# A graph layer on one core: gathered columns tied to TensorE's progress

## The chip, the cores and the metric

The kernel runs on one core of one Trainium2 chip. The metric is device time in microseconds of one execution, as the median of repeated runs. The page and the trace describe one profiled execution of the same program.

## The reference

One layer of a graph network with 6,250 nodes of 64 features and 206,250 edges, whose end nodes `dst` are sorted. For each edge the normalised row of its source node is added to the edge's attributes, the sum goes through a relu, and the results are summed by end node; then come two small matrix products.

```python
h = jnp.maximum(_layernorm(x, axis=-1), 0.0)
msg = jax.nn.relu(h[src] + edge_attr)
agg = jax.ops.segment_sum(msg, dst, num_segments=x.shape[0])
g = h + agg
g = jax.nn.relu(g @ W1 + b1)
return x + (g @ W2 + b2)
```

## The kernel before

The edges are cut into 269 groups (`NG` = 268 full ones and a tail) of 128 partitions by 6 columns (`G`), so a group holds 768 edges. Each edge needs the row of its source node, and the kernel gets these rows in two ways. Three of a group's six columns (`G - H`) are fetched by GpSimd: `gather` issues one indirect DMA for each column, which takes 128 rows of `h_rows` (the normalised nodes, in DRAM) by the indices in `src_sb`, into a tile `xg`. The other three columns (`H`) are worked out by TensorE from a copy of all nodes that stays on the chip (`hp`): `find` and `back` (VectorE, with a part on ScalarE) build 0/1 tables, `slots_of` (L487) multiplies them with `hp` into a half bank, `slots_out` (L495, ScalarE) copies the result to `picked`, and `pick` (L502) sorts the rows to the edges in a PSUM bank, on top of the attributes that `room` (L510) has copied there. Twelve groups (`WHOLE`) have all six columns done by TensorE; they are two units each and nothing is gathered for them. All other groups from the sixth on (`F0` = 5) are one unit. The first five groups are gathered in full.

`half(u)` issues one unit: it enters the group `AHEAD` = 9 groups later (`enter`, `load`: the attributes by SP's DMA queue, the gathered columns by GpSimd's), then `window_sum(u - 1)` (L600, the sums by node of the unit before), `room`, three calls of `slots_of` for the next set (20, 16 and 16 matmuls of L487) with two `slots_out`, `pick(u + 1)` (18 matmuls of L502), `sum_into_z` (L563), `messages` (L585 adds the gathered columns to the attributes, L588 adds up the picked ones, L590 is the relu), the third `slots_out`, and the one-hot of L569 by which `window_sum` sums. A set is two units, so which `slots_of` comes in which unit is written out by hand. Preparations for later sets (`rank_at`, `rank_count`, `rank_of`, `rank_turn`, `source`) are spread over the units by `chunk`.

The schedule is manual: each engine executes its instructions in the order in which they are issued in the code, and an instruction waits by semaphores only for what it reads and overwrites. GpSimd's queue holds nearly nothing but gathers, so before the change a gather waits only for its turn, for its indices and rows, and for its `xg` tile (twelve of them), whose last reader is L585. GpSimd thus works ahead of the other engines as far as there are free tiles.

Before the units comes a stage that normalises the nodes (`ln_head`, `ln_rows`, `ln_turn`, `ln_parts`) and a loop over the first five groups, which are entered, added, summed by node, and mixed with the first preparations: `rank_count` (L279 and L281, counts, copied by L283), `source` (L331, copied by L334) and `window_sum`.

Of the kernel before, what the change touches and what calls it, by code (L numbers as in the profile page):

```python
# [19 lines left out]
N, E, D = 6250, 206250, 64  # L20
P = 128
G = 6
# [17 lines left out]
AHEAD = 9  # L40
# [4 lines left out]
H = 3  # L45
PP, RR = 128, 49
# [4 lines left out]
S = 32  # L51
J = P // S
assert PARTS * BB == RR - 1 and PP == P and PARTS % J == 0
Q = PARTS * S // P
# [3 lines left out]
RAW = 3  # L58
F0 = 5
# [22 lines left out]
def kernel(  # L82
# [14 lines left out]
    nc = tc.nc  # L97
# [9 lines left out]
    src_sb = const.tile([P, CP], I32, name="src_sb")  # L107
# [56 lines left out]
    ones_b = const.tile([P, P], F16, name="ones_b")  # L164
# [13 lines left out]
    hp = const.tile([PP, RR, 3, D], BF16, name="hp")  # L178

    h_rows = dram.tile([NP, D], F32, name="h_rows")  # L180
# [14 lines left out]
                              in_=edge_attr[C * P:(C + TJ) * P, :].rearrange("(p j) d -> p (j d)", j=TJ))  # L195
            nc.sync.dma_start(out=ea[:, G - 1, :], in_=edge_attr[E - P:, :])

    def gather(xg, idx, n, rows):
        for j in range(n):
            nc.gpsimd.indirect_dma_start(  # L200
                out=xg[:, j, :], out_offset=None, in_=rows[:, :],
                in_offset=bass.IndirectOffsetOnAxis(ap=idx[:, j:j + 1], axis=0))

    def first_col(g):
        return 0 if g < NG else G - CT
# [4 lines left out]
    def pool_cols(g):  # L210
        return G if g < F0 else 0 if is_whole(g) else G - H

    def load(g):
        ea = eas[g % LOOK]
        attr_load(ea[:, :G], g)
        lo, hi = first_col(g), pool_cols(g)
        if is_whole(g):
            return ea, None
        if g < F0:
            xg = lnp.tile([P, G, D], F32, name="xr", bufs=F0)  # L220
        else:
            xg = edge.tile([P, G - H, D], F32, name="xg")
        gather(xg[:, lo:], src_sb[:, g * G + lo:g * G + hi], hi - lo, x if g < RAW else h_rows)
        return ea, xg

    loaded = [load(g) for g in range(RAW)]
# [49 lines left out]
    def rank_count(c):  # L276
        ps = psum.tile([P, RG, PARTS, H], F32, name="rows", bufs=1)
        at = ats[c]
        nc.tensor.matmul(ps, upper, at, start=True, stop=False)  # L279
        for d in range(1, H):  # L280
            nc.tensor.matmul(ps[:, :, :, d:], ones_b, at[:, :, :, :H - d], start=False, stop=(d == H - 1))  # L281
        counts[c] = rank.tile([P, RG, PARTS, H], F16, name="before", bufs=1)
        nc.scalar.copy(counts[c], ps)  # L283

# [39 lines left out]
    def source(c):  # L324
        n = RG // 2
        ps = psum.tile([n * S, 2, n * S], F32, name="rows", bufs=1)
        mk, oh = marks.pop(c), holds.pop(c)
        for u in range(2):
            for t in range(H):
                row = lambda a: a[:, u * n:(u + 1) * n, :, t].rearrange("p g s -> p (g s)")  # L330
                nc.tensor.matmul(ps[:, u], row(mk), row(oh), start=(t == 0), stop=(t == H - 1))  # L331
        col = rank.tile([PARTS, RG * S], I16, name="source")
        for i in range(n):
            nc.scalar.copy(col.rearrange("m (u i s) -> m u i s", u=2, s=S)[:, :, i],  # L334
                           ps[i * S:i * S + PARTS, :, i * S:(i + 1) * S])
        lines[c] = dram.tile([SETS, PARTS, 2 * S], I16, name="source_row", bufs=3)
        nc.sync.dma_start(out=lines[c].rearrange("k m s -> m k s"), in_=col.rearrange("m (k s) -> m k s", k=SETS))
# [101 lines left out]
    backs, sources, spots, found, picked, halves, picks = {}, {}, {}, {}, {}, {}, {}  # L439

    def source_load(k):
        sources[k] = rank.tile([P, PARTS * 2 * S], I16, name="sources")
        nc.sync.dma_start(out=sources[k][:PP], in_=lines[k // SETS][k % SETS].rearrange("(o m) s -> o (m s)", o=1)
                          .to_broadcast([PP, PARTS * 2 * S]))
# [34 lines left out]
    def slots_of(k, n0):  # L479
        ps = next_half()[:, :2 * 3 * D].rearrange("p (u d) -> p u d", u=2)  # L480
        for u in range(2):
            i, q = divmod(n0 + u, Q)
            sets = BB + 1 if q == 0 else BB
            for b in range(sets):
                for j in range(J):
                    m = (b * PARTS + q * J) + j if b < BB else BB * PARTS + j
                    nc.tensor.matmul(ps[j * S:(j + 1) * S, u], found[k][:, m, i, :],  # L487
                                     hp[:, min(m, RR - 1)].rearrange("p t d -> p (t d)"),
                                     start=(b == 0), stop=(b == sets - 1))
        if n0 == 0:  # L490
            picked[k] = hot.tile([P, 2 * Q, 3 * D], BF16, name="picked")
        halves[k, n0] = ps

    def slots_out(k, n0):
        nc.scalar.copy(picked[k][:, n0:n0 + 2], halves.pop((k, n0)))  # L495

    def pick(u0, cols):
        k, i = divmod(u0, 2)
        ps = picks[u0]
        for u in cols:  # L500
            for q in range(Q):
                nc.tensor.matmul(ps[:, u, :3].rearrange("p t d -> p (t d)"), backs[k][:, q, i * H + u, :],  # L502
                                 picked[k][:, i * Q + q], start=False, stop=(q == Q - 1), skip_group_check=True)

    def room(u):
        g, c0 = UNITS[u]
# [54 lines left out]
    def sum_into_z(u):  # L561
        at = window_start(group_of(u))
        nc.vector.tensor_tensor(z[:, ds(at, W)], z[:, ds(at, W)], aggs.pop(u), ALU.add)  # L563
# [7 lines left out]
            slots.unsqueeze(1).to_broadcast([P, n, W]), ALU.is_equal)  # L571
        hots[u] = oh

    def enter(g):
        if g <= NG and g not in taken:
            taken[g] = loaded[g] if g < RAW else load(g)

    def messages(u):
        g, (lo, hi) = group_of(u), span(u)
# [15 lines left out]
    def window_sum(u):  # L595
        (lo, hi), oh, msg = span(u), hots.pop(u), msgs.pop(u)
        pa = half_banks[u % 3][:, 2 * 3 * D + u // 3 % AB * W:][:, :W]
        for j in range(lo, hi):
            i = (j - lo) % 2
            nc.tensor.matmul(pa[i * D:(i + 1) * D], msg[:, j, :], oh[:, j, :], start=(j < lo + 2), stop=(j >= hi - 2))  # L600
        aggs[u] = pa

    xbs = {}
# [57 lines left out]
    def half(u):  # L661
        g = group_of(u)
        k, i = divmod(u, 2)
        first = ((0, 2), (6, 8))[i]
        later = ((4,), (10,))[i]
        now = is_set(k + 1)
        if is_first(u):
            enter(g + AHEAD)
        if i == 0:
            if is_set(k + 3):  # L670
                source_load(k + 3)
        elif is_set(k + 3):
            spot_load(k + 3)
        window_sum(u - 1)
        if u + 1 < U:
            room(u + 1)
        if now:
            for n0 in first:
                slots_of(k + 1, n0)
                slots_out(k + 1, n0)  # L680
            for n0 in later:
                slots_of(k + 1, n0)
        if u + 1 < U:
            pick(u + 1, range(H))
        sum_into_z(u - LAG)
        blocks_behind(u - LAG)
        messages(u)
        if now:
            for n0 in later:
                slots_out(k + 1, n0)  # L690
        one_hot(u)
        if i == 0:
            if is_set(k + 1):
                back_near(k + 1)
                back(k + 1, 3, Q)
            if is_set(k + 2):
                find(k + 2, 0)
                find(k + 2, BB)
        else:
            if is_set(k + 2):  # L700
                back_far(k + 2)
                back(k + 2, 0, 3)
                find(k + 2, 1)
        chunk(u + 14, rank_at)
        chunk(u + 13, rank_count)
        chunk(u + 12, rank_of)
        chunk(u + 11, rank_marks)
        chunk(u + 11, rank_turn)
        chunk(u + 10, rank_holds)
        chunk(u + 10, rank_fits)  # L710
        chunk(u + 9, source)
        if g in CHECKS and is_first(u):
            find_left(CHECKS.index(g))
# [50 lines left out]
    slots_of_edges()  # L764
    ln_turn(*rows[-1])
    rank_fits(0)
    for g in range(AHEAD):
        enter(g)
    places(2, NCH)
    for k in (0, 1):  # L770
# [3 lines left out]
    for g in range(F0):  # L774
        for i in range(g * LOOK // F0, (g + 1) * LOOK // F0):
            tails_begin(i)
        enter(g + AHEAD)
        messages(g - F0)
        one_hot(g - F0)
        if g == 0:  # L780
            rank_at(1)
            rank_count(1)
        if g == 1:
            rank_of(1)
            rank_marks(1)
            rank_turn(1)
        if g == 2:
            rank_holds(1)
            rank_fits(1)
            source(1)  # L790
        if g == 3:
            rank_at(2)
            rank_count(2)
        if g >= 1:
            window_sum(g - 1 - F0)
        if g > LAG:
            sum_into_z(g - LAG - 1 - F0)
    sum_into_z(-LAG - 1)
    while split:
        fill()  # L800
# [6 lines left out]
    back(0, 0, Q)  # L807
    back_near(0)
    for n0 in range(0, 2 * Q, 2):
        slots_of(0, n0)  # L810
        slots_out(0, n0)
    source_load(2)
    spot_load(2)
    room(0)
    pick(0, range(H))
    for b in range(BB + 1):
        find(1, b)
    back_far(1)
# [87 lines left out]
```

## Time and profile before

| | us |
|---|---|
| median of 3 runs | 1706.47 |
| lowest, highest run | 1706.32, 1710.89 |
| profiled execution | 1700.59 |
| its span, from the first to the last instruction | 1698.9 |
| TensorE matmuls busy | 1226.6 (72%) |
| TensorE weight loads busy | 957.5 (56%) |
| VectorE busy | 995.5 (59%) |
| ScalarE busy | 954.9 (56%) |
| GpSimd busy | 785.4 (46%) |
| mean granted TensorE clock | 0.914 |

The busy times come from the first part of the page. PE is TensorE's matmuls, PEld its weight loads, DVE VectorE, ACT ScalarE, POOL GpSimd and SP SyncE. In the rows, a line such as L585 is the line of the kernel that issued the instruction. "<-" behind the idle time of an instruction names what ended the wait before it; "issue" is time in which nothing that the profile shows was waited for, and "remote" a signal that the profile cannot put down to an instruction. In a timeline row, neighbouring instructions of one kind are merged and counted with x.

### The profile page before, as it was taken

What the parts mean: (1) busy time and instruction counts of PE and PEld (TensorE: products, weight loads), DVE (VectorE), ACT (ScalarE), POOL (GpSimd) and SP (SyncE); (2) the same over time, 40 slices, a digit from 0 to 9 for tenths busy, and PEclk for the clock granted to TensorE, in tenths of its full rate; (3) what the DMA queues carried; (4) which work ended last, traced back from release to release, by engine and by line L of the source; (5) the groups of instructions that cost most, each with busy time, mean ns of one, the idle gap of its engine ahead of it and who ended that gap; (6) DMA issues with size and microseconds to landing.
All of it is one profiled execution on the core that took longest, in us unless ns stands there. A gap on an engine that the chain in (4) does not pass through costs nothing. (4 is left out here: it accounts for less than half of the span.)

```text
span 1698.9 us, 54613 instructions
## 1 busy us (share of the span) xinstructions
PE 1226.6 (72%) x23185; PEld 957.5 (56%) x23185; DVE 995.5 (59%) x2686; ACT 954.9 (56%) x1979; POOL 785.4 (46%) x798
## 2 busy tenths in 40 slices
PE   3047777777777777877777777777777777777786
PEld 2036565655556566656556555655655565565665
DVE  7446556656566555655656555655556555565565
ACT  4335555556556555555655655655555555565664
POOL 6734544553453543554455454444444544545510
PEclk8569999899999998899999999988999999999998
DMA  5213433334333433334333433433334333434330
GB/s 182 70 51 104 110 96 105 108 96 111 102 97 107 112 104 93 107 94 118 105 104 102 109 103 98 105 106 103 96 102 106 98 106 106 109 98 109 106 95 25
DMA packets 115095, 172.34 MB, mean 101 GB/s; under 512 B 28444, under 2 KB 83613, under 8 KB 114845
## 3 DMA queue, kind: packets, MB, share of 16 engines
q1 hardware_dynamic: 89752, 143.03, 28.2%
q0 software_dynamic: 25088, 25.74, 8.5%
q8 instruction: 184, 3.01, 0.7%
q14 instruction: 67, 0.54, 0.1%
q10 hardware_dynamic: 4, 0.01, 0.0%
HBM read 164.85 MB, written 3.84 MB: 99 GB/s over the span
## 5 line engine op out<-in xcount | busy, mean ns | idle before, releaser
L200 POOL DMA_INDIRECT xg<-h_rows,src_sb x754 | 749.9, 995 | 827.6 <-DVE ea L585 662.4
L487 PE MATMUL half<-hp,found 128*32 128x192 bf16 x14352 | 509.6, 256 | 267.3 <-issue 243.3
L495 ACT CAST picked<-half 128x384 bf16<-128x384 f32 x828 | 365.2, 475 | 344.3 <-PE half L487 300.2
L487 PEld LDWEIGHTS <-found 128*32 128x32 bf16 x14352 | 325.2, 98 | 393.6 <-issue 357.1
L502 PE MATMUL pick<-picked,backs 128*128 128x192 bf16 x4968 | 519.1, 266 | 3.5 <-ACT pick L510 2.1
L502 PEld LDWEIGHTS <-backs 128*128 128x128 bf16 x4968 | 449.3, 106 | 60.5 <-issue 50.7
L563 DVE TENSOR_TENSOR z<-z,half 128x32 f32 x281 | 53.0, 189 | 638.4 <-ACT picked L495 511.1
L590 ACT ACTIVATE msg<-ea 128x384 f32<-128x384 f32 (+2 forms) x281 | 142.9, 509 | 259.2 <-DVE ea L588 199.1
L474 DVE TENSOR_SCALAR backs<-spots,ids 128x768 bf16<-128x768 int16 x690 | 279.9, 453 | 0.0
L600 PE MATMUL half<-oh,msg 128*64 128x32 f32 x3224 | 152.7, 229 | 109.5 <-ACT picked L495 57.5
L600 PEld LDWEIGHTS half<-oh,msg 128*64 128x64 f32 x3224 | 121.3, 140 | 171.8 <-ACT picked L495 75.1
L455 DVE TENSOR_SCALAR found<-sources,nodes_of 128x1536 bf16<-128x1536 int16 (+1 forms) x414 | 211.4, 537 | 0.1
L588 DVE TENSOR_REDUCE ea<-pick 128x192 f32<-128x576 f32 x276 | 207.1, 750 | 0.1
L510 ACT COPY pick<-ea 128x576 f32<-128x576 f32 x264 | 168.4, 638 | 0.0
L467 ACT ACTIVATE backs<-dist,ones 128x768 bf16<-128x768 bf16 x138 | 129.3, 937 | 0.3 <-ACT dist L464 0.3
L464 ACT ACTIVATE dist<-spots,far 128x768 bf16<-128x768 int16 x138 | 129.2, 936 | 0.0
L569 DVE TENSOR_TENSOR oh<-slot,slots 128x192 f32<-128x192 int16 (+2 forms) x281 | 95.4, 340 | 36.9 <-remote 36.9
L585 DVE TENSOR_TENSOR ea<-ea,xg 128x192 f32<-128x192 f32 x252 | 90.0, 357 | 1.8 <-issue 1.3
L279 PE MATMUL rows<-at,upper 128*128 128x432 f16 x46 | 16.5, 358 | 49.1 <-remote 28.4
L283 ACT CAST before<-rows 128x432 f16<-128x432 f32 x46 | 23.4, 510 | 35.7 <-remote 31.8
L331 PE MATMUL rows<-holds,marks 128*96 128x96 f16 x276 | 25.9, 232 | 11.4 <-DVE oh L569 5.0
L334 ACT CAST source<-rows 24x64 int16<-24x64 f32 x138 | 27.5, 199 | 8.5 <-remote 5.3
(107 smaller groups left out, 439.7 us busy)
## 6 DMA issues: line engine op xcount, KB each, us to landing
sources<-source_row SPq DMA_DIRECT2D x138, 384.0 KB
ea<-in_edge_attr_dram SPq DMA_DIRECT2D x268, 192.0 KB
spots<-spot_rows SPq DMA_DIRECT2D x138, 192.0 KB
xg<-h_rows,src_sb POOLq DMA_INDIRECT x754
xb<-in_x_dram SPq DMA_DIRECT2D x12, 128.0 KB
out_dram<-o SPq DMA_DIRECT2D x12, 128.0 KB
h_rows<-x SPq DMA_DIRECT2D x3, 384.0 KB
dst_sb<-in_dst_main_dram SPq DMA_DIRECT2D x1, 804.0 KB
```

Of the source, the lines that this page charges most:

```text
L200: nc.gpsimd.indirect_dma_start(out=xg[:, j, :], out_offset=None, in_=rows[:, :], in_offset=bass.IndirectOffsetOnAxis(ap=idx[:, j:j + 1], a ...
L455: nc.vector.tensor_scalar(found[k][:, b * PARTS:b * PARTS + n].rearrange("p m i s -> p (m i s)"), sources[k][:, :n * 2 * S], nodes_of[:, b ...
L464: nc.scalar.activation(dists[k], spots[k].bitcast(I16), AF.Abs, bias=far)
L467: nc.scalar.activation(backs[k][:, Q - 1].rearrange("p t s -> p (t s)"), dists.pop(k), AF.Relu, bias=ones[:, 0:1], scale=-1.0)
L474: nc.vector.tensor_scalar(backs[k][:, q].rearrange("p t s -> p (t s)"), spots[k].bitcast(I16), ids[:, q:q + 1], None, op0=ALU.is_equal)
L487: nc.tensor.matmul(ps[j * S:(j + 1) * S, u], found[k][:, m, i, :], hp[:, min(m, RR - 1)].rearrange("p t d -> p (t d)"), start=(b == 0), st ...
L495: nc.scalar.copy(picked[k][:, n0:n0 + 2], halves.pop((k, n0)))
L502: nc.tensor.matmul(ps[:, u, :3].rearrange("p t d -> p (t d)"), backs[k][:, q, i * H + u, :], picked[k][:, i * Q + q], start=False, stop=(q ...
L510: nc.scalar.copy(picks[u][:, :H, :3], parts)
L588: nc.vector.tensor_reduce(ea[:, c0:c0 + H], picks.pop(u)[:, :H, :3].rearrange("p j t d -> p j d t"), AX.X, ALU.add)
L590: nc.scalar.activation(msg[:, lo:hi], ea[:, lo:hi], AF.Relu)
L600: nc.tensor.matmul(pa[i * D:(i + 1) * D], msg[:, j, :], oh[:, j, :], start=(j < lo + 2), stop=(j >= hi - 2))
```

## The change

The list `beats` collects matmul instructions of TensorE as they are issued. `gather` takes a tuple `behind` of such instructions, and ties its last `len(behind)` columns to them, one each: the indirect DMA of a column waits for its matmul's completion. In the units, `half(u)` enters group `g + 9` with the last three marks: the end of the first `slots_of`, the end of the third, and the end of the `pick` of the unit before. Before the units, groups 0 to 6 are entered at once without waits (before: 0 to 8), and groups 7 to 13 one or two at the end of each pass of the loop over the first five groups, with their last two columns behind the last two marks of that time: counts, sources and sums by node. Groups 14 and later are entered by the units as before, now with marks.

```diff
+    beats = []
+    beat = mybir.DependencyInfo(mybir.DependencyClass.Sync, mybir.DependencyReason.ANTI)
+
+    def gather(xg, idx, n, rows, behind=()):
         for j in range(n):
-            nc.gpsimd.indirect_dma_start(
+            it = nc.gpsimd.indirect_dma_start(
...
+            if j >= n - len(behind):
+                tc.add_manual_dep(it.ins, behind[j - n + len(behind)].ins.name, beat, reason="pace")
...
 (rank_count) if c < 3: beats.append(last)
 (source)     if c < 2: beats.append(last)
 (window_sum) if u < -1: beats.append(last)
...
-    def enter(g):
+    def enter(g, behind=()):
         if g <= NG and g not in taken:
-            taken[g] = loaded[g] if g < RAW else load(g)
+            taken[g] = loaded[g] if g < RAW else load(g, behind[first_col(g):])
...
         if is_first(u):
-            enter(g + AHEAD)
+            enter(g + AHEAD, beats[-G + H:])
...
             for n0 in first:
-                slots_of(k + 1, n0)
+                begun = slots_of(k + 1, n0)
                 slots_out(k + 1, n0)
+                if n0 == first[0]:
+                    beats.append(begun)
             for n0 in later:
-                slots_of(k + 1, n0)
+                beats.append(slots_of(k + 1, n0))
         if u + 1 < U:
-            pick(u + 1, range(H))
+            beats.append(pick(u + 1, range(H)))
...
-    for g in range(AHEAD):
+    for g in range(F0 + 2):
         enter(g)
...
-        enter(g + AHEAD)
         messages(g - F0)
...
         if g > LAG:
             sum_into_z(g - LAG - 1 - F0)
+        for e in ((7,), (8,), (9,), (10, 11), (12, 13))[g]:
+            enter(e, beats[-2:])
...
     for n0 in range(0, 2 * Q, 2):
-        slots_of(0, n0)
+        begun = slots_of(0, n0)
         slots_out(0, n0)
+        if n0 % 4 == 0 and n0:
+            beats.append(begun)
...
-    pick(0, range(H))
+    beats.append(pick(0, range(H)))
```

The three lines in brackets stand for the same step in three functions, which also keep their last matmul in `last`; `slots_of` and `pick` return theirs.

## The prediction

> **What bounds the kernel now.** The page comes first: no engine is full (TensorE is busy 72% of the span), so the time is in the waits. The row that stands out is GpSimd's:
>
> ```profile
> span 1698.9 us, 54613 instructions
> L200 POOL DMA_INDIRECT xg<-h_rows,src_sb x754 | 749.9, 995 | 827.6 <-DVE ea L585 662.4
> ```
>
> 754 gathers of about 1 us, which start when VectorE's addition of L585 has freed a tile. I then took one unit from the timeline. Columns: start, length, engine, line, operation, and in brackets the idle time before it and what ended it.
>
> ```profile
> 601.20 1.66 PE L502 MATMUL pick<-picked,backs 128*128 128x192 bf16 x18
> 602.13 0.94 POOL L200 DMA_INDIRECT xg<-h_rows,src_sb  x1 [1.86 <-DVE ea L585]
> 603.14 0.54 PE L600 MATMUL half<-oh,msg 128*64 128x32 f32 x12 [0.27 <-issue]
> 603.37 1.02 POOL L200 DMA_INDIRECT xg<-h_rows,src_sb  x1 [0.30 <-issue]
> 603.61 0.90 PE L487 MATMUL half<-hp,found 128*32 128x192 bf16 x32
> 604.70 0.95 POOL L200 DMA_INDIRECT xg<-h_rows,src_sb  x1 [0.30 <-issue]
> 604.98 0.29 PE L487 MATMUL half<-hp,found 128*32 128x192 bf16 x3 [0.47 <-issue]
> 605.72 0.24 PE L487 MATMUL half<-hp,found 128*32 128x192 bf16 x1 [0.45 <-issue]
> 606.44 0.85 PE L487 MATMUL half<-hp,found 128*32 128x192 bf16 x16 [0.48 <-issue]
> 606.58 0.86 ACT L495 CAST picked<-half 128x384 bf16<-128x384 f32 x2 [1.76 <-PE half L487]
> 607.09 0.19 DVE L563 TENSOR_TENSOR z<-z,half 128x32 f32 x1 [1.65 <-ACT picked L495]
> 607.22 2.71 PE L502 MATMUL pick<-picked,backs 128*128 128x192 bf16 x18
> 607.27 0.36 DVE L585 TENSOR_TENSOR ea<-ea,xg 128x192 f32<-128x192 f32 x1
> 607.90 0.94 POOL L200 DMA_INDIRECT xg<-h_rows,src_sb  x1 [2.25 <-DVE ea L585]
> ...
> 610.63 0.95 POOL L200 DMA_INDIRECT xg<-h_rows,src_sb  x1 [0.31 <-issue]
> ...
> 612.45 0.86 ACT L495 CAST picked<-half 128x384 bf16<-128x384 f32 x2 [1.54 <-PE half L487]
> ```
>
> Three gathers run back to back (602.13, 603.37, 604.70). TensorE starts the 52 matmuls of L487 at 603.61, breaks off after 32, and does the last 16 only at 606.44. The first copy of L495 needs the first 20 of the 52, which are over by 604.51, yet it begins at 606.58, 1.88 us after the third gather began. In the next unit it begins at 612.45, 1.82 us after that unit's third (610.63). VectorE (L563, L585) and the next gathers follow from that copy, so it closes the loop. The counter-example is a whole group, for which nothing is gathered:
>
> ```profile
> 151.92 0.75 DVE L588 TENSOR_REDUCE ea<-pick 128x192 f32<-128x576 f32 x1
> 153.57 1.26 PE L487 MATMUL half<-hp,found 128*32 128x192 bf16 x52
> 154.74 0.85 ACT L495 CAST picked<-half 128x384 bf16<-128x384 f32 x2
> 155.79 0.75 DVE L588 TENSOR_REDUCE ea<-pick 128x192 f32<-128x576 f32 x1
> ...
> 148.04:155.79 7.75, 7.25 (x161) 6.17 (x160) 6.33 (x19) 6.19 (x13) 0.00 (x0) 1.00 0.34 97
> ...
> L588 DVE TENSOR_REDUCE ea<-pick x262: 748/750/759, 118.8 to 1628.5; 128x192 f32<-128x576 f32 x131
> L200 POOL DMA_INDIRECT xg<-h_rows,src_sb x718: 939/946/1286, 119.1 to 1628.9; - x180
> ```
>
> Here the 52 matmuls are one run and the two units without gathers take 7.75 us together, 3.88 each (window row: start:end, length, busy times by engine). The last two rows (one line's instructions from 118 us on) give the mean: 261 units between 118.8 and 1628.5, of which 718/3 = 239 with three gathers and 22 without; (1509.7 - 22 x 3.88)/239 = 5.96 us. So three gathers go with 2.08 us more per unit, 497 us in all. That is the bound I go by: a series of gathers keeps back TensorE's signals, and some of its instructions, until about 1.85 us after its last one began.
>
> The same stands in the stage before the units, where 36 gathers ran one after the other:
>
> ```profile
> 52.64 0.95 POOL L200 DMA_INDIRECT xg<-h_rows,src_sb  x1 [0.30 <-issue]
> 62.20 0.86 PE L600 MATMUL half<-oh,msg 128*64 128x32 f32 x12
> 69.48 0.94 POOL L200 DMA_INDIRECT xg<-h_rows,src_sb  x1 [0.30 <-issue]
> 90.54 0.36 DVE L569 TENSOR_TENSOR oh<-slot,slots 128x192 f32<-128x192 int16 x1 [28.43 <-remote]
> 91.72 0.80 PE L281 MATMUL rows<-at,ones_b 128*128 128x288 f16 x2
> 97.00 0.95 POOL L200 DMA_INDIRECT xg<-h_rows,src_sb  x1 [0.30 <-issue]
> 100.34 0.52 ACT L283 CAST before<-rows 128x432 f16<-128x432 f32 x1 [31.83 <-remote]
> 109.03 3.27 PE L487 MATMUL half<-hp,found 128*32 128x192 bf16 x68 [13.25 <-DVE found L455]
> ```
>
> The sums by node of L600 are through at 63.06, but the one-hot that needs their buffer starts at 90.54, 27.5 us later; the counts of L281 are through at 92.52, their copy starts at 100.34.
>
> But not every signal is late:
>
> ```profile
> 609.14 1.18 POOL L200 DMA_INDIRECT xg<-h_rows,src_sb  x1 [0.30 <-issue]
> 609.86 0.23 PE L317 MATMUL rows<-ident_b,spot_i 128*18 128x128 bf16 x1
> 610.12 0.26 ACT L319 COPY sp<-rows 18x128 bf16<-18x128 bf16 x1
> ...
> 1628.87 0.95 POOL L200 DMA_INDIRECT xg<-h_rows,src_sb  x1 [2.33 <-DVE ea L585]
> ...
> 1631.39 1.26 PE L487 MATMUL half<-hp,found 128*32 128x192 bf16 x52
> ```
>
> Between a unit's second and third gather, 0.98 us after the second began, a signal arrives at once (609.86 + 0.23, used at 610.12). Behind the only gather that stands alone (1628.87), the 52 run unbroken. So the hold comes late in a series: after about two gathers, until 1.85 us past the last.
>
> **The change part by part.** *In the units.* Nothing is computed more or less; three matmuls a unit gain a signal and each gather waits for one. Column 0 waits for the first 20 matmuls of L487, column 1 for the last 16, column 2 for the pick of L502, all of the unit before. These gathers get into tiles freed two groups earlier (12 tiles, now fetched ten groups ahead), so L585 no longer releases them. Call the moment of the first L495 copy T (606.58). Today the first gather starts at 607.90, T + 1.32. From the end of L585 (607.63) to that start it takes 0.27 us; the same after a TensorE signal, and 0.03 for a second wait instruction, makes T + 0.30. The signals of columns 1 and 2 do not delay their gathers: the last 16 end at 607.29, T + 0.7, the pick (0.64 after T, 1.66 long) at T + 2.3, while GpSimd, at the spacing of 602.13 to 604.70, comes to the third only at T + 0.30 + 2.57 = T + 2.87. So the series stays back to back but begins 1.02 us earlier in the unit. The hold then ends at T + 2.87 + 1.85 = T + 4.72, later than the 3.88 a unit needs by itself, so it still sets the unit. Today the same sum is 1.32 + 2.57 + 1.85 = 5.74 against 5.78 measured (606.58 to the next T would be 5.87). Gain: 1.02 x 239 = 244 us.
>
> Bounds of this term: if the hold disappears, a unit is 3.88 plus the addition of L585, 0.36, that whole groups lack: 4.24, a gain of 1.72 x 239 = 411. If picks stay as slow as at 607.22 (2.71 instead of 1.66), the pick ends at T + 3.35, the third gather starts at T + 3.65, and the unit is 5.50: a gain of 0.46 x 239 = 110. I take the middle value since 1.66 is the pick behind an unheld stretch. The granted clock was 1.00 in the stretch without gathers. The Trainium skill (TensorE: Matmul & The Clock Gate, "What's actually happening") halves the clock after an idle window of about 3.4 us; by that rule no unit, before or after, would have the slow pick and the sum is 244; the row of 2.71 behind gaps far shorter than that speaks against relying on it.
>
> *What waits behind it.* On GpSimd only gathers are queued, so a waiting gather delays gathers alone; their reader, L585, comes ten groups later, 47 us at 4.7 us. SP's queue keeps its order in the units; before them the loads of groups 7 to 13 come after those of sources and spots, free, since they are needed from the third unit on.
>
> *Before the units.* Groups 7 to 13 (10 is whole) are entered one by one with columns 1 and 2 behind TensorE's last two marks; groups 14 to 17 move into the units. GpSimd would run as now up to column 1 of group 9 (69.48), then wait for the very sums of L600 started at 62.20. The series stops, the hold ends at 69.48 + 1.85 = 71.3, and the one-hot of 90.54 starts 19.2 us earlier. The counts end 2.0 us later (73.3); two gathers (71.6, 72.85) hold them to 74.7, 1.4 us instead of 7.8: 6.4 more. From the copy (100.34) to the first unit work (109.03) lies real work, unchanged. Sum 25 us, between 0 and 26. The 12 gathers moved into the units make four more units of the gathered kind: 4 x (4.94 - 3.88) = 4 us back, 4.94 being 5.96 - 1.02.
>
> Sum: the profiled execution took 1700.6 us (span 1698.9 + 1.7); 1700.6 - 244 - 25 + 4 = 1436. The median of the runs, 1706.5, lies 0.35% above it. I say 1430.
>
> **The rivals.** *Spread, they hold nothing* (0.16): waits put enough room between gathers that each behaves like that of 1628.87. For: that row. Against: by the sum above GpSimd is the late one and the series stays closed. 1700.6 - 411 - 21 = 1268.
>
> *The hold moves along* (0.13): it is paid per gather wherever it begins, the units stay at 5.96, only the stage before them gains: 1680. For: 2.08/3 = 0.69 us per gather, near the gaps of 0.7 us between the starts at 604.98, 605.72 and 606.44. Against: the unheld 52 at 1631.39.
>
> *Gathers wait for their own hold* (0.15), slower: if a single gather keeps back TensorE's signal for the full 1.85 us, each next column can start only 1.85 + 0.30 after the one before. A unit becomes 0.30 + 2 x 2.15 + 1.85 = 6.45, 0.49 more in 243 units: +119 - 25 = 1795. It decides once the hold begins less than 0.4 us after a gather starts (the last 16 signal at T + 0.7). Against: the signal at 610.09 came through 0.95 us into one.
>
> *The order of gathers is nothing to TensorE* (0.04): its gaps come from its own issue, as their label says, and both stages stay: 1700. The Trainium skill (SBUF — State Buffer, "SBUF: two separate sides") has TensorE on ports of its own, waiting on nobody, which speaks for this. The units of 3.88 us speak against it.
>
> **How the numbers follow.** The forecast has 0.52, its own range 1330 (units of 4.5) to 1570 (slow picks). The rivals have 0.16, 0.13, 0.15, 0.04. From 1255 to 1685 the range holds the forecast and the first two rivals, 0.81. Faster by over 0.3% (about what a measurement of this kernel can tell): 0.52 + 0.16 + 0.13 = 0.81; within 0.3%: 0.04; slower: 0.15.
>
> **What would show it.** Right: gathers released by PE L487 and L502 rather than L585; the first of a unit about 0.3 us after the L495 copy begins; units near 4.7 us; L487 still broken, but shorter; L495 still some 1.85 us behind the third gather; first L487 near 84 us instead of 109; picks mostly 1.66. Wrong: units at 3.9 to 4.3 with unbroken runs of 52 (first rival), at 5.8 (second), or above 6 with GpSimd idle between columns for 2 us (third).

## The result and the profile after

| | before | after |
|---|---|---|
| median of 4 runs, us | 1706.39 | 1530.7 |
| lowest to highest, us | 1702.1 to 1710.89 | 1529.74 to 1531.52 |
| span of the profiled execution, us | 1698.9 | 1528.6 |
| mean granted TensorE clock | 0.914 | 0.945 |

The ratio after to before is 0.897, 95% interval 0.8946 to 0.8994. The change gains 176 us where 276 were forecast: the time lies inside the range, 101 us above the number. The direction held; one step of the mechanism behind the number, as the experiments will show, did not.

The lines of the code have moved: the gather is now L204, `slots_of` L497, `slots_out` L506, `pick` L513, the addition into `z` L575, the addition of the gathered columns L597, the reduction L600, the sums by node L612. From the page after (busy time, mean ns of one, idle time before it and what ended most of it):

```profile
span 1528.6 us, 55110 instructions
L204 POOL DMA_INDIRECT xg<-h_rows,src_sb x754 | 746.1, 990 | 678.6 <-PE half L497 552.5
L497 PE MATMUL half<-hp,found 128*32 128x192 bf16 x14352 | 442.1, 256 | 112.6 <-issue 57.9
L513 PE MATMUL pick<-picked,backs 128*128 128x192 bf16 x4968 | 486.4, 255 | 3.5 <-ACT pick L522 2.1
```

Gathers are now released by `slots_of` on TensorE instead of the addition on VectorE. Where the time went is read from one line of the source view in each kernel: the reduction that each unit makes once, with its first and its last start. Before:

```profile
L588 DVE TENSOR_REDUCE ea<-pick x276: 748/750/759, 118.8 to 1687.5; 128x192 f32<-128x576 f32 x138
```

After:

```profile
L600 DVE TENSOR_REDUCE ea<-pick x276: 743/750/758, 98.8 to 1517.2; 128x192 f32<-128x576 f32 x138
```

The first unit starts its reduction 20.0 us earlier, and the 275 distances between the reductions take 1418.4 us instead of 1568.7, 150.3 less; together this is the 170.3 us by which the spans differ. A mean unit (whole groups included) went from 5.70 to 5.16 us. One unit of the timeline after:

```profile
480.26 0.70 PE L497 MATMUL half<-hp,found 128*32 128x192 bf16 x24 [0.47 <-issue]
480.47 0.86 ACT L506 CAST picked<-half 128x384 bf16<-128x384 f32 x2 [0.99 <-PE half L497]
480.71 0.95 POOL L204 DMA_INDIRECT xg<-h_rows,src_sb  x1 [1.00 <-PE half L497]
480.89 1.66 PE L513 MATMUL pick<-picked,backs 128*128 128x192 bf16 x18
482.38 0.95 POOL L204 DMA_INDIRECT xg<-h_rows,src_sb  x1 [0.72 <-PE half L497]
483.11 0.54 PE L612 MATMUL half<-oh,msg 128*64 128x32 f32 x12 [0.56 <-DVE backs L484]
483.58 0.76 PE L497 MATMUL half<-hp,found 128*32 128x192 bf16 x27
483.63 1.21 POOL L204 DMA_INDIRECT xg<-h_rows,src_sb  x1 [0.30 <-issue]
485.25 0.57 PE L497 MATMUL half<-hp,found 128*32 128x192 bf16 x17 [0.47 <-issue]
485.45 0.48 ACT L506 CAST picked<-half 128x384 bf16<-128x384 f32 x1 [0.66 <-PE half L497]
```

Take 480.47 as T, the start of the first copy. Column 0 starts at T + 0.24. The third `slots_of` ends at 480.96, but column 1, which waits for it, starts only at 482.38, T + 1.91; back to back with column 0, as the forecast had it, it would have started at about T + 1.54. Column 2 follows at T + 3.16. The next copy comes at 485.45, 1.82 us after the third gather, although its 20 matmuls were over by 484.34: the unit takes 4.98 us. So a single gather already holds back a signal, and the room that this makes between the first gather and the second is new.

### The profile page after: what moved, and what is told of

Same layout as the page of the kernel before. It is cut to its first block, busy times and chain, and to the rows that moved or that the text cites. A ratio compares the mean times of both kernels' runs of the same rounds, so it can differ in the third digit from the quotient of the medians.

```text
span 1528.6 us, 55110 instructions
## 1 busy us (share of the span) xinstructions
PE 1131.4 (74%) x23185; PEld 915.9 (60%) x23185; DVE 981.6 (64%) x2686; ACT 951.2 (62%) x1979; POOL 780.3 (51%) x798
## 5 line engine op out<-in xcount | busy, mean ns | idle before, releaser
L204 POOL DMA_INDIRECT xg<-h_rows,src_sb x754 | 746.1, 990 | 678.6 <-PE half L497 552.5
L497 PE MATMUL half<-hp,found 128*32 128x192 bf16 x14352 | 442.1, 256 | 112.6 <-issue 57.9
L513 PE MATMUL pick<-picked,backs 128*128 128x192 bf16 x4968 | 486.4, 255 | 3.5 <-ACT pick L522 2.1
L513 PEld LDWEIGHTS <-backs 128*128 128x128 bf16 x4968 | 421.7, 102 | 54.0 <-issue 50.5
L506 ACT CAST picked<-half 128x384 bf16<-128x384 f32 x828 | 365.8, 475 | 110.0 <-PE half L497 105.1
L497 PEld LDWEIGHTS <-found 128*32 128x32 bf16 x14352 | 312.1, 99 | 187.3 <-issue 102.3
L575 DVE TENSOR_TENSOR z<-z,half 128x32 f32 x281 | 52.9, 188 | 508.2 <-ACT picked L506 429.0
L612 PE MATMUL half<-oh,msg 128*64 128x32 f32 x3224 | 151.5, 228 | 208.4 <-ACT msg L602 84.1
L612 PEld LDWEIGHTS half<-oh,msg 128*64 128x64 f32 x3224 | 120.1, 139 | 274.3 <-ACT msg L602 164.7
L484 DVE TENSOR_SCALAR backs<-spots,ids 128x768 bf16<-128x768 int16 x690 | 260.0, 425 | 0.0
L600 DVE TENSOR_REDUCE ea<-pick 128x192 f32<-128x576 f32 x276 | 206.6, 749 | 0.1
L465 DVE TENSOR_SCALAR found<-sources,nodes_of 128x1536 bf16<-128x1536 int16 (+1 forms) x414 | 198.9, 507 | 0.1
L597 DVE TENSOR_TENSOR ea<-ea,xg 128x192 f32<-128x192 f32 x252 | 93.9, 373 | 1.4 <-issue 1.0
L339 PEld LDWEIGHTS <-marks 128*96 128x96 f16 x276 | 23.1, 147 | 14.2 <-issue 7.2
```

Of the source, the lines that this page charges most:

```text
L204: it = nc.gpsimd.indirect_dma_start(out=xg[:, j, :], out_offset=None, in_=rows[:, :], in_offset=bass.IndirectOffsetOnAxis(ap=idx[:, j:j + ...
L465: nc.vector.tensor_scalar(found[k][:, b * PARTS:b * PARTS + n].rearrange("p m i s -> p (m i s)"), sources[k][:, :n * 2 * S], nodes_of[:, b ...
L484: nc.vector.tensor_scalar(backs[k][:, q].rearrange("p t s -> p (t s)"), spots[k].bitcast(I16), ids[:, q:q + 1], None, op0=ALU.is_equal)
L497: last = nc.tensor.matmul(ps[j * S:(j + 1) * S, u], found[k][:, m, i, :], hp[:, min(m, RR - 1)].rearrange("p t d -> p (t d)"), start=(b == ...
L513: last = nc.tensor.matmul(ps[:, u, :3].rearrange("p t d -> p (t d)"), backs[k][:, q, i * H + u, :], picked[k][:, i * Q + q], start=False, ...
L600: nc.vector.tensor_reduce(ea[:, c0:c0 + H], picks.pop(u)[:, :H, :3].rearrange("p j t d -> p j d t"), AX.X, ALU.add)
```

## The experiments

All ratios are to the kernel before on the same chip. "Mean unit" is the distance between the first and the last reduction of that kernel, divided by 275. The rows come from several chips, and where "1 run" stands the time is that of a single execution.

| kernel | median us | before us | ratio | first reduction | mean unit |
|---|---|---|---|---|---|
| whole change | 1530.7 | 1706.39 | 0.897 | 98.8 | 5.16 |
| units_only | 1541.32 | 1704.1 | 0.905 (0.9022 to 0.9079) | 108.7 | 5.15 |
| before_only | 1693.34 | 1704.1 | 0.9935 (0.9911 to 0.996) | 112.6 | 5.70 |
| all_first | 1707.14 | 1704.1 | 1.0014 (0.9991 to 1.0038) | 99.5 | 5.80 |
| all_pick | 1878.11 | 1704.1 | 1.1045 (1.1002 to 1.1088) | 97.4 | 6.33 |
| none_gathered | 1300.14 (1 run) | 1672.87 | 0.777 | 94.9 | 4.34 |
| one_gathered | 1383.54 (1 run) | 1672.87 | 0.827 | 96.1 | 4.64 |
| two_gathered | 1397.44 (1 run) | 1672.87 | 0.835 | 97.2 | 4.68 |
| sums_second_pick | 1507.35 | 1672.87 | 0.9002 (0.8982 to 0.9022) | 97.1 | 5.11 |
| after_sums_late | 1471.01 | 1703.39 | 0.8641 (0.8617 to 0.8665) | 94.8 | 4.96 |
| all_first_sums_late | 1610.36 | 1703.39 | 0.9457 (0.943 to 0.9485) | 95.4 | 5.47 |
| one_sums_late | 1231.26 (1 run) | 1703.39 | 0.723 | 94.4 | 4.09 |
| before_sums_late | 1164.8 | 1313.27 | 0.8868 (0.8853 to 0.8883) | 78.4 | 3.93 |

**The two halves.** units_only puts the stage before the units back:

```diff
-    for g in range(F0 + 2):
+    for g in range(AHEAD):
         enter(g)
...
+        enter(g + AHEAD)
         messages(g - F0)
...
-        for e in ((7,), (8,), (9,), (10, 11), (12, 13))[g]:
-            enter(e, beats[-2:])
```

> The waits in the units alone; the stage before the units fetches as the kernel before does. If the two halves of the change are independent, the first reduction of a unit is back at about 119 us (99 with the whole change) and the time is the whole change's 1531 plus 20, near 1550. If the early gain is only handed on to a later wait, it is 1531 to 1535.

before_only takes the waits out of the units:

```diff
-            enter(g + AHEAD, beats[-G + H:])
+            enter(g + AHEAD)
```

> The waits before the units alone; in the units the gathers are released by the addition, as in the kernel before. Independent halves: first reduction near 99 us, units at 5.9 us again, 1706 - 20 = 1686. If the units profit from the different start, less than 1680; if the gain is lost again in them, 1700 to 1706.

units_only gains 163 us, before_only 11; the whole ratio of 0.897 would be 176 us on this chip. The halves nearly add up, and the units carry the change. The first reductions were not as expected: that of units_only was to be back at 119 us and comes at 108.7, and the early half by itself brings it forward by 6 us, not by 20. TensorE's timeline of before_only shows why:

```profile
81.15 2.46 PE L497 MATMUL half<-hp,found 128*32 128x192 bf16 x46 [4.70 <-DVE found L465]
83.82 0.33 PE L497 MATMUL half<-hp,found 128*32 128x192 bf16 x1 [0.21 <-issue]
...
102.34 0.32 PE L497 MATMUL half<-hp,found 128*32 128x192 bf16 x1 [1.77 <-issue]
103.75 0.35 PE L497 MATMUL half<-hp,found 128*32 128x192 bf16 x2 [1.08 <-issue]
104.44 1.42 PE L497 MATMUL half<-hp,found 128*32 128x192 bf16 x27 [0.34 <-issue]
106.99 3.04 PE L513 MATMUL pick<-picked,backs 128*128 128x192 bf16 x18 [1.12 <-ACT pick L522]
```

and so does GpSimd's in the same stretch:

```profile
81.47 0.94 POOL L204 DMA_INDIRECT xg<-h_rows,src_sb  x1 [0.30 <-issue]
...
100.42 0.94 POOL L204 DMA_INDIRECT xg<-h_rows,src_sb  x1 [0.30 <-issue]
112.98 0.94 POOL L204 DMA_INDIRECT xg<-h_rows,src_sb  x1 [11.62 <-DVE ea L597]
```

The first `slots_of` starts 27.9 us earlier than in the kernel before (109.03 there), and then the gathers that were fetched later, now without waits, run back to back from 81.47 to 101.36 across it. After the first 46 matmuls, TensorE's come in ones, twos and threes, 0.7 to 2.8 us apart, until 104.44: 31 matmuls in 20.8 us. It is the clearest picture of the hold in the case: TensorE has work, waits for nothing that the profile shows, and is let on in small steps while GpSimd gathers without a pause. With the whole change these gathers wait for `slots_of` too. The view by windows (length, busy times by engine, granted clock, DMA) has the price of it once more:

```profile
81.15:104.44 23.29, 7.87 (x77) 3.58 (x78) 4.73 (x13) 1.24 (x3) 15.34 (x17) 0.50 0.32 83
```

TensorE is busy for 7.87 of 23.29 us and runs at half its clock; the pick of 106.99 takes 3.04 us. The Trainium skill (TensorE: Matmul & The Clock Gate, "What's actually happening") says that the clock is halved until TensorE has been busy for a window of about 3.4 us; the granted clock of 0.50 in this row agrees.

**The placement that the forecast had in mind.** all_first ties all three columns to the first mark, all_pick all three to the last:

```diff
-            enter(g + AHEAD, beats[-G + H:])
+            enter(g + AHEAD, [first] * 3)      # all_pick: [pick] * 3
```

> All three columns of a group wait for the same mark, the first 20 matmuls of slots_of, so that the three gathers run back to back from 0.3 us after it, which is the placement that the prediction had in mind. Theory A (the hold ends 1.8 us after the last gather of a closed series, and the late third slots_of, held back by the first gather, is what made the change worth less): units 0.3 + 2.5 + 1.8 = 4.6 to 4.7 us instead of 5.3, 243 x 0.65 = 160 us faster than the whole change, near 1370. Theory B (it is the room between the gathers that made the change's gain): back-to-back gathers hold longer, units 5.7 us, 1620. Theory C (a fixed price per gather): no change, 1530.

> All three columns wait for the last mark of a unit, the pick. Theory A with the hold's end setting the unit: the series starts 2.0 us later than behind the first mark, its hold ends at 2.55 + 2.5 + 1.8 = 6.85 us after the first mark, units 6.5 to 6.9 us, 1820 to 1910. If the series can lie anywhere and its hold only stretches the unit to its own length, 0.3 + 2.5 + 1.8 = 4.6 to 5 us, 1360 to 1450. Theory C (a fixed price per gather): 5.3 us, 1530.

all_first starts its series earlier in the unit than the kernel before (in the unit below 0.23 us behind the first copy, against 1.32) and runs it back to back, which is the placement that the forecast summed up, and on balance it gains nothing (1.0014). Theory A, the forecast's own, had 1370 us and does not hold. A unit from its timeline:

```profile
454.88 0.86 ACT L506 CAST picked<-half 128x384 bf16<-128x384 f32 x2
455.11 0.94 POOL L204 DMA_INDIRECT xg<-h_rows,src_sb  x1 [6.47 <-PE half L497]
456.36 0.94 POOL L204 DMA_INDIRECT xg<-h_rows,src_sb  x1 [0.30 <-issue]
457.51 0.71 PE L612 MATMUL half<-oh,msg 128*64 128x32 f32 x12 [0.44 <-DVE backs L484]
457.61 1.05 POOL L204 DMA_INDIRECT xg<-h_rows,src_sb  x1 [0.30 <-issue]
458.16 0.26 PE L497 MATMUL half<-hp,found 128*32 128x192 bf16 x2
459.44 0.99 PE L497 MATMUL half<-hp,found 128*32 128x192 bf16 x37 [1.02 <-issue]
460.08 0.48 ACT L506 CAST picked<-half 128x384 bf16<-128x384 f32 x1 [0.21 <-PE half L497]
```

The third gather begins at 457.61, so by the forecast's rule the next copy should come 1.85 us later, at 459.46. At that moment (459.44) TensorE has only just been let on; it broke off after 2 of the 52 matmuls, and the copy needs 20: it comes at 460.08, 5.20 us after the last one. Here it is TensorE's own instructions that are late, not only a signal. The units of all_first differ much, which a table below takes up. Its mean granted clock is also lower (0.882, against 0.914 before and 0.945 after the change), and how much of its time that makes was not separated. all_pick, where the series lies 2 us later in the unit, ends inside theory A's first range (1820 to 1910), though A is not its only explanation.

**The price of a gather.** From group 14 on some columns come by a plain transfer of consecutive rows instead:

```diff
+        if g >= 14 and n == H:          # m: columns not gathered, 3, 2 or 1
+            nc.sync.dma_start(out=xg[:, H - m:]..., in_=h_rows[r0:r0 + P * m, :]...)
+            hi = lo + H - m
+            behind = behind[:H - m]
         gather(xg[:, lo:], ..., behind)
```

> From group 14 on nothing is gathered: the three columns come by one plain transfer of consecutive rows on SP's queue (other rows than the reference's, the same bytes). It gives the floor of a unit in which GpSimd does nothing. All theories: units at 3.9 (whole groups) to 4.24 (with the addition), 1531 - 243 x (5.33 - 4.05 to 4.24) = 1220 to 1265. If the units stay above 4.6, something other than the gathers sets them.

> From group 14 on only column 0 is gathered, behind the first mark; columns 1 and 2 come by a plain transfer of consecutive rows (not the reference's). Theory D (a gather holds TensorE's signals from the first tenths of a microsecond after its start until 1.42 us after it, and a unit grows only by holds that reach a signal its loop waits for): the hold ends 1.7 us after the first mark, before the loop needs TensorE again, so as without gathers, at most 25 us more, 1220 to 1290; the signal of the third slots_of comes 1.0 us late, at 1.7 after the first mark. Theory C (a fixed price per gather, 0.45 us of the 1.3): +110, near 1350. The prediction's reading (the hold comes after about two gathers): no late signal at all.

> From group 14 on columns 0 and 1 are gathered, behind the first and the third slots_of; column 2 comes by a plain transfer (not the reference's rows). Theory D: the second gather starts 1.95 us after the first mark and its hold ends at 3.4; the sums by node and the next 20 matmuls (0.7 us) come behind it or in it, so units 4.2 to 4.5, 1265 to 1330. Theory C: +220 over none, near 1450. The prediction's reading: the two holds nothing, as without gathers.

The first column costs 83 us, the second 14, by single executions; three columns would take 0.897 x 1672.87 = 1501 us on this chip (worked out, not run), 103 more. It is no fixed price per gather (theory C), but theory D did not foresee the 83 either. The timelines show it. Without gathers, from the last of the `slots_of` matmuls (L505 in these kernels) over the copies (L514) and the addition into `z` (L583) to the reduction (L608):

```profile
353.88 1.00 PE L505 MATMUL half<-hp,found 128*32 128x192 bf16 x40
354.49 0.87 ACT L514 CAST picked<-half 128x384 bf16<-128x384 f32 x2
354.99 0.19 DVE L583 TENSOR_TENSOR z<-z,half 128x32 f32 x1 [1.34 <-ACT picked L514]
355.36 0.75 DVE L608 TENSOR_REDUCE ea<-pick 128x192 f32<-128x576 f32 x1
```

The same unit with column 0 gathered:

```profile
373.69 1.00 PE L505 MATMUL half<-hp,found 128*32 128x192 bf16 x40
374.31 0.87 ACT L514 CAST picked<-half 128x384 bf16<-128x384 f32 x2
374.32 0.95 POOL L204 DMA_INDIRECT xg<-h_rows,src_sb  x1 [3.60 <-PE half L505]
375.81 0.19 DVE L583 TENSOR_TENSOR z<-z,half 128x32 f32 x1 [2.35 <-ACT picked L514]
376.19 0.75 DVE L608 TENSOR_REDUCE ea<-pick 128x192 f32<-128x576 f32 x1
```

The 40 matmuls, which end with the third `slots_of`, are over at 354.88 and at 374.69. VectorE's addition into `z` starts 0.11 us behind their end without a gather and 1.12 us behind it with one, and the reduction goes with it. The addition into `z` reads a sum that lies in the same PSUM bank as a half of `slots_of`, and I read these rows as a wait for the third `slots_of`, although the brackets name ScalarE's copy. The trace settles it, since it also keeps the times at which TensorE's semaphore count (the signal of its finished matmuls) goes up. For these matmuls that is 354.90 and 375.73, and in both kernels the addition starts 0.08 us behind such a rise in nearly every third unit (88 and 91 of 92). So one lone gather, started 0.37 us before those matmuls ended, holds their signal for 1.0 us, until the gather is 1.4 us old.

The same count shows it throughout. From the eleventh unit on, TensorE gives 983 signals in each of the two kernels. Without gathers none comes more than 0.03 us behind the end of its matmul; with column 0 gathered 242 come over 0.3 us late, and 236 of these when the gather is 1.35 to 1.45 us old. In the kernel before, most late ones come 1.6 to 1.95 us after the last gather's start.

Because three banks rotate, the wait falls in every third unit. There the distance between reductions is 0.96 us longer with column 0 gathered, 87 us over the whole kernel, and the other units together are 5 us shorter: the 83 us are this wait. Since a set is two units, the pattern repeats every six. The medians of the distances by their place in it, in us:

| kernel | 1 | 2 | 3 | 4 | 5 | 6 |
|---|---|---|---|---|---|---|
| before | 5.75 | 6.08 | 5.70 | 5.78 | 6.06 | 5.56 |
| whole change | 4.02 | 5.14 | 5.96 | 4.55 | 5.05 | 5.95 |
| all_first | 3.97 | 5.91 | 6.99 | 4.55 | 5.80 | 6.84 |
| none_gathered | 3.87 | 4.42 | 3.57 | 4.47 | 4.24 | 4.25 |
| one_gathered | 3.87 | 4.42 | 4.57 | 4.47 | 4.24 | 5.23 |

At places 3 and 6 the addition into `z` waits for the third `slots_of`. The whole change brings places 1 and 4 nearly down to what they take without gathers, 2 and 5 about 1 us down, and 3 and 6 not at all. all_first has the short places 1 and 4 as well and loses them again at 3 and 6: its 1.0014 is a balance.

**Room, or the place of the marks.** sums_second_pick has a mark of its own for each column, but other ones:

```diff
-            enter(g + AHEAD, beats[-G + H:])    # first, third slots_of, pick
+            enter(g + AHEAD, [sums, second, pick])
```

> All three columns are kept, each behind a mark of its own, but earlier ones: column 0 behind the sums by node (0.7 us ahead of the first slots_of), column 1 behind the second slots_of, column 2 behind the pick. If room between the gathers is all that counts (theory B), the time stays at 1531. Theory D: the first gather now holds the signal of the first slots_of itself, until 1.42 us after its start, which is 1.0 us later than it came; column 1 follows at 0.3 after that, the pick and column 2 about 2.1 after that, and its hold ends 1.42 later: units 5.5 (5.3 to 5.8), 1531 + 243 x 0.2 = 1575 (1530 to 1645). Theory A (the end of the last hold only, series seen from its start): the series starts 0.7 us earlier, units 4.6, 1360.

0.9002 against 0.897: as good as the same (theory B), where D's 1575 us would be 0.92 and A's 1360 us 0.80; D's range began at 1530 us, so it is not excluded. The earlier mark did not bring the series forward: the signal of the sums by node is itself held back by the gathers before it (in one unit the sums are over at 483.16, and column 0 starts at 485.77). In these runs it counts that gathers are not all back to back, and hardly which of TensorE's signals is between them.

**The addition into z out of the way.** Moved behind the one-hot in VectorE's order:

```diff
-        sum_into_z(u - LAG)
-        blocks_behind(u - LAG)
         messages(u)
...
         one_hot(u)
+        sum_into_z(u - LAG)
+        blocks_behind(u - LAG)
```

> The whole change, and VectorE's addition of the sums into z is moved from ahead of the unit's reduction to behind its one-hot. Theory D2: a first gather alone keeps back the third slots_of's signal for 1.0 us, and in every third unit the addition into z waits for just that signal (same bank), ahead of the reduction in VectorE's order; so units of 5.4 us (one in three to six) become 5.0 like the others: 25 to 35 us of 1531, ratio to the kernel before 0.88. Rival: T is set by the last gather's hold in any case, and nothing moves: ratio 0.897.

> All columns behind the first mark (ratio 1.00 to the kernel before), and the addition into z moved behind the one-hot. Theory D2: with the series closed, the signals of the second and third slots_of come up to 4 us late, and the addition into z and so the reduction wait for them in the long units (6 to 7.4 us); out of the reduction's way, each unit is 2.75 + 1.85 + 0.6 = 5.2 us, set by the hold of TensorE's own instructions: 0.6 us less per unit, ratio 0.91. Rival: it is the instructions that are held, not this signal: ratio 1.00.

> Only column 0 gathered (ratio 0.827 to the kernel before; columns 1 and 2 by a plain transfer, not the reference's rows), and the addition into z moved behind the one-hot. Theory D2: the 0.35 us per unit that the lone gather costs is that wait, 1.0 us in every third unit, so all of it goes: ratio 0.777 as without gathers. Rival: the gather costs it in another way: 0.827.

after_sums_late beats both kernels: 1471.01 us, ratio 0.8641, by the ratios 3.7% under the whole change, more than the 25 to 35 us expected. Its timeline shows a unit in which the gathers alone set the end:

```profile
475.39 0.86 ACT L506 CAST picked<-half 128x384 bf16<-128x384 f32 x2 [0.56 <-PE half L497]
475.63 0.94 POOL L204 DMA_INDIRECT xg<-h_rows,src_sb  x1 [1.12 <-PE half L497]
477.35 0.94 POOL L204 DMA_INDIRECT xg<-h_rows,src_sb  x1 [0.78 <-PE half L497]
478.02 0.75 DVE L600 TENSOR_REDUCE ea<-pick 128x192 f32<-128x576 f32 x1
478.11 0.92 PE L497 MATMUL half<-hp,found 128*32 128x192 bf16 x27
478.59 0.94 POOL L204 DMA_INDIRECT xg<-h_rows,src_sb  x1 [0.30 <-issue]
480.44 0.86 ACT L506 CAST picked<-half 128x384 bf16<-128x384 f32 x2 [1.48 <-remote]
```

The next 27 matmuls are over at 479.03, the reduction has long run, and the copy still waits until 480.44, 1.85 us after the third gather. The unit is 0.24 + 1.72 + 1.24 + 1.85 = 5.05 us: the start of column 0, its own hold and the way to column 1, the spacing, the last hold. all_first gains 0.056 by the same move, which fits its long places 3 and 6, but 0.9457 is far from 0.91; whether the rest is held instructions or the lower clock (0.896) was not separated. With the move in both, the opening between the gathers is still worth 139 us on this chip (1610.36 against 1471.01), so the wait of the addition is not all that it saves. one_sums_late is no clean measure, since it is faster than none_gathered (0.723 against 0.777): the move is worth something without any gather too, and its gains are not a measure of the hold alone.

**The kernel before with the same move.**

> The kernel before, without any of the new waits, and the addition into z moved behind the one-hot, which takes it out of the way of the addition that releases the gathers. If room between the gathers is what the change gains by (theory D2), a closed series that begins earlier gains little: units 5.4 to 5.9 instead of 5.96 and the early stage unchanged, ratio to the kernel before 0.92 to 1.00, well above the 0.864 of the whole change with the same move. If the wait of the addition into z was the whole loss, the new waits are not needed: ratio 0.86 or less.

This run came onto a chip that behaves differently: the kernel before took 1313.27 us there (7 runs, 1310.54 to 1314.7), 393 us less than in the first runs. The timeline of before_sums_late has gathers back to back and next to no hold:

```profile
387.05 0.94 POOL L200 DMA_INDIRECT xg<-h_rows,src_sb  x1 [0.30 <-issue]
388.14 0.48 ACT L495 CAST picked<-half 128x384 bf16<-128x384 f32 x1
388.30 0.99 POOL L200 DMA_INDIRECT xg<-h_rows,src_sb  x1 [0.30 <-issue]
389.57 1.26 PE L487 MATMUL half<-hp,found 128*32 128x192 bf16 x52
389.59 1.25 POOL L200 DMA_INDIRECT xg<-h_rows,src_sb  x1 [0.31 <-DVE backs L474]
390.22 0.86 ACT L495 CAST picked<-half 128x384 bf16<-128x384 f32 x2 [0.23 <-PE half L487]
```

The 52 matmuls run in one piece while the third gather of a series begins, and the copy follows 0.63 us after that gather's start instead of 1.85. By the count, 39 of 1212 signals come over 0.3 us late in this run. The kernel before left no timeline on this chip; that it is not held there either is taken from its time. So 0.8868 says that the move is worth 11% where hardly anything is held, and nothing on whether the new waits are needed where something is. Whether the change gains on such a chip, and what the kernel before with the move gains on a chip that holds, was not tried.

## Why the prediction was right, and where it was wrong

*The bound* was right: gathers hold TensorE back, and without them the units take 4.34 us (none_gathered). The 497 us put down to them were too many, since units without gathers were taken at 3.88 us: none_gathered saves 373 us (1672.87 to 1300.14), a part of it before the units. The end of the hold, 1.85 us after the last gather, was right in size: 1.82 and 1.85 in the two units above.

*The step that failed* is "So the hold comes late in a series: after about two gathers". It rested on one signal that came through between two gathers (609.86 in the kernel before), and on the lone gather of 1628.87, behind which the 52 matmuls run unbroken. But these start 2.52 us after that gather, later than the end of any hold quoted here, so this row could not tell. Why the signal of 609.86 came through, 0.95 us into a gather, stays open. In one_gathered a lone gather holds a signal that is due 0.4 us after its start for 1.0 us. From this step came "the signals of columns 1 and 2 do not delay their gathers": in the unit after the change the matmuls of column 1's mark end at T + 0.49 and their signal arrives at T + 1.65 (482.12 by the count) instead of the forecast's T + 0.7, its gather starts at T + 1.91, column 2 at T + 3.16, and the hold ends at T + 4.98 instead of T + 4.72.

*The term of 244 us* measured 150 (5.70 to 5.16 us per mean unit). That difference looks like a mis-sized term, but all_first shows that the reasoning behind it does not hold: the assumed placement, a closed series 1 us earlier, gives 1.0014. The sum also has no term for the addition into `z`, which waits for the held signal of the third `slots_of` at places 3 and 6, where the change gains nothing. It gains at the others: the timelines show column 0's own hold pushing column 1 away, which opens a stretch in which signals and instructions get through, and all_first and sums_second_pick show that the gain goes with that opening. That 1430 us was said where the sum is 1436, and the median lies 0.35% above the profiled execution, is a slip: carried through, the forecast is 1441. The first rival had the cause nearest (room between the gathers), but not its size, since room for one signal is not an end of the hold. The third rival had the mechanism (a gather waits for its predecessor's hold), with 1.4 us instead of 1.85 and for one column only, so it does not turn the sign. The fourth, that the order is nothing to TensorE, which stood beside the Trainium skill's statement that TensorE's ports wait on nobody (SBUF — State Buffer, "SBUF: two separate sides"), is contradicted by before_only's row of 102.34 and by the two units. On the last chip the 52 matmuls run unbroken, as that statement would have it; whether TensorE's ports have a part in the hold no run here shows.

*The stage before the units* was forecast at 25 us. The first L497 was to begin near 84:

```profile
83.43 0.35 PE L497 MATMUL half<-hp,found 128*32 128x192 bf16 x4 [4.70 <-DVE found L465]
```

25.6 us earlier than before, as forecast; but the first reduction comes only 20.0 us earlier. What was left out is that gathers which no longer run then run later, across the first `slots_of`: six of them start between 82.65 and 90.58.

*Picks* were to be mostly 1.66 us; the mean matmul of a pick went from 266 to 255 ns, and the pick quoted after the change (480.89) takes 1.66. Of the 276 picks 247 take at most 1.75 us, but 220 did so before.

## What to carry to other kernels

When one engine's instructions seem to slow another's, space them before moving them: here three gathers back to back make a mean unit of 5.7 to 5.8 us, whether the series begins 1 us earlier or not, and of 5.2 with one opening between them. A signal that arrives in time once does not show that nothing is held before it: take the suspected instructions out one at a time and read where each signal lands. A wait that sits ahead of the critical instruction in an engine's order without belonging to it (here the addition into `z`) is worth moving even if it looks short: here it took the ratio from 0.897 to 0.8641.

## What was not expected of the hardware

- A single gather of 0.95 us keeps a signal of TensorE until it is about 1.4 us old; three in a series keep the next until 1.82 to 1.85 us after the last one's start.
- Under gathers back to back TensorE executed 31 matmuls in 20.8 us (before_only), in steps of about 0.7 us or a few times that. What holds its instructions and signals the traces do not show.
- The hold is not the same on all chips. In the runs whose kernel before took 1673 to 1706 us it was there; where it took 1313 us hardly any of it was, in the one timeline from there (before_sums_late). A tuning that spaces gathers is therefore only shown for chips of the first kind.
